# Adding the feed-forward's last bias: four GpSimd additions per group, or one accumulating DMA

## The chip, the core and the metric

The kernel runs on one core of a Trainium2 chip. The core has five engines that run their own instruction streams and wait for each other through semaphores: PE (TensorE, matmuls; its weight loads are listed apart as PEld), DVE (VectorE), ACT (ScalarE), POOL (GpSimd) and SP (SyncE, which here only issues DMAs). Sixteen DMA engines move data between HBM and SBUF. A DMA is issued either by SP, on a queue that the hardware serves, or by POOL, on a queue whose descriptors GpSimd's own software writes. The metric is the device time of one execution in microseconds (us), the median of several runs.

## What is computed

Two layers, each a graph convolution and a feed-forward, over 32 graphs of 512 nodes with 256 features, in float32. The change is in the first layer's feed-forward. Cut to what matters, with `xx` a token's normalized features:

```python
t = max over d of (xx[d] + Wt[f, d]) + bt[f]          # "tropical" product, f = 0..1023
trop = s * max_k(t * sl_cvx + of_cvx) + (1 - s) * min_k(t * sl_ccv + of_ccv)
classical = gelu(xx @ Wc + bc)
g = sigmoid(xx @ Wg + bg)
fused = g * trop + (1 - g) * classical
x = x + (fused @ Wd + bd)
```

The last bias `bd` has 256 numbers. In these inputs they are all zero, and both kernels add them all the same.

## The kernel before

The first layer (`layer0_sorted`) works in four segments of eight graphs, 4096 tokens or 32 tiles of 128 tokens each. Its idea: the maximum over `d` is mostly decided by a token's few largest features. So for each token the graph convolution writes one row to HBM (`rows_of`, 275 numbers: the 256 features, the norm's shift and scale, a count, and the eight largest features with their places). Tokens are then sorted by how many candidates they need. The feed-forward takes the tokens in that order, in groups of four tiles, eight groups per segment, 32 groups in all. Tile number n of a segment looks at `CAPS[n]` candidates: 24, 9, 7, 6, 5, 5, 5, then 4, 3, 2 and 1. Group g takes the tiles g, g+8, g+16 and g+24.

Each group goes through three functions:

- `sums` (from L546) gathers the four tiles' rows into the SBUF tile `xs` (variable `xg`, shape 128 x 4 x 275, three buffers; L553), normalizes the features into `xn` on ACT (L574), turns them on PE for the matmuls, and gathers for each candidate one 4 KB row of the table per token (`best` at L564 for the first candidate, `rows` at L595 for the others). DVE folds each into the running maximum (L598). At its end it compares the counts (`over`, L606) and adds the bias `bd` to the features in `xs`, in four additions on GpSimd, one per tile (L609 and L610). `bd` is a constant in SBUF, the bias repeated in all 128 partitions, loaded once at the start.
- `mixed` does the two matmuls into `cls` and `gate` (L623), their activations (L625) and the mixing of both with the tropical part, on PE, ACT and DVE (L630 to L641).
- `down` multiplies with `Wd` (L652), adds the product on DVE to what stands in `xs` (L654), and stores the features to HBM from SP (`x2s`, L655).

`sums` of a group is woven with `mixed` of the group before, and `down` of that group comes after the first step of the next `mixed`. Beside both runs the graph convolution of the later segments, and in the last segment the start of the second layer. Its work stands on the same engines: on POOL it issues the loads of the adjacency matrix (`adj`, L392) and does small operations for the norms (L30, L31) and copies into the row (L453, L454, L465, L466).

The order of instructions on each engine is not the program's order: the framework simulates the program and puts each engine's instructions in the order in which it expects them to become ready. In the profile the four additions of one group are therefore not next to each other on POOL; gathers and small operations stand between them. A buffer's reuse and every read after a write are guarded by semaphores that the framework places.

The lines that matter: `bd` at L141, `sums` with L553, L564, L574, L595, L598, L606, L609 and L610, and `down` with L654 and L655. The constants are all issued by one helper at L135, so the profile shows that line for them.

Of the kernel before, what the change touches and what calls it, by code (L numbers as in the profile page):

```python
# [8 lines left out]
F32 = mybir.dt.float32  # L9
# [5 lines left out]
ALU = mybir.AluOpType  # L15
# [4 lines left out]
P = 128  # L20
N = 512
D = 256
NT = N // P
# [74 lines left out]
def layer0_sorted(tc, ident, eps, x, adj, w, x2s, ranks, over, following):  # L98
# [6 lines left out]
    nc = tc.nc  # L105
# [22 lines left out]
    with ExitStack() as ctx:  # L128
        cst = ctx.enter_context(tc.tile_pool(name="c0", bufs=1))
        dr = ctx.enter_context(tc.tile_pool(name="d0", bufs=2, space=DRAM))  # L130
        ps = ctx.enter_context(tc.tile_pool(name="p0", bufs=2, space=PSUM))

        def const(name, shape, src):
            t = cst.tile(shape, F32, tag=name, name=name)
            nc.sync.dma_start(t, src)  # L135
            return t
# [1 line left out]
        w_msg = const("w_msg", [P, DC, D], w["W_msg"].rearrange("(c p) u -> p c u", p=P))  # L138
        w_upd = const("w_upd", [P, DC, D], w["W_upd"].rearrange("(c p) u -> p c u", p=P))
        bias = const("bias", [P, D], w["bias"].partition_broadcast(P))  # L140
        bd = const("bd", [P, D], w["bd"].partition_broadcast(P))  # L141
        wc = cst.tile([P, DC, FFN], F32, tag="wc", name="wc")
        wg = cst.tile([P, DC, FFN], F32, tag="wg", name="wg")
        wd = cst.tile([P, FC, D], F32, tag="wd", name="wd")
# [29 lines left out]
        for c in range(CT // P):  # L174
            nc.gpsimd.affine_select(below[:, c, :], below[:, c, :], pattern=[[1, CT]], compare_op=ALU.is_gt,
                                    fill=0.0, base=-c * P, channel_multiplier=-1)

        table = dr.tile([D, FFN], F32, tag="table", name="table", bufs=1)
        least = dr.tile([2, D], F32, tag="least", name="least", bufs=1)
        rows_of = [dr.tile([ST * P, RW], F32, tag=f"rows_of{i}", name=f"rows_of{i}", bufs=1) for i in range(len(x2s))]  # L180
# [362 lines left out]
        def feed_forwards():  # L543


            def sums(s, g):  # L546

                tiles = range(g, ST, NG)
                while s not in placed_segs:
                    next(ahead)  # L550
                xg = sb.tile([P, NT, RW], F32, tag="xs", name=f"xs{s}_{g}", bufs=3)
                for t, tile_no in enumerate(tiles):
                    nc.gpsimd.indirect_dma_start(  # L553
                        out=xg[:, t, :], out_offset=None, in_=rows_of[s],
                        in_offset=bass.IndirectOffsetOnAxis(
                            ap=order[:, s * ST + tile_no : s * ST + tile_no + 1].bitcast(U32), axis=0))
                xnT = sb.tile([P, DC, N], F32, tag="xnT", name=f"xnT{s}_{g}")
                pt = [ps.tile([P, NT, P], F32, tag="tp", name=f"xsp{s}_{g}_{c}") for c in range(DC)]
                best = []

                def ask(t):

                    best.append(sb.tile([P, FFN], F32, tag="best", name=f"best{s}_{g}_{t}", bufs=2 * NT - 1))
                    nc.gpsimd.indirect_dma_start(  # L564
                        out=best[t], out_offset=None, in_=table,
                        in_offset=bass.IndirectOffsetOnAxis(ap=xg[:, t, IDX : IDX + 1].bitcast(U32), axis=0))

                ask(0)
                for t, tile_no in enumerate(tiles):
                    if t + 1 < NT - 1:  # L570
                        ask(t + 1)
                    r, cap = xg[:, t, :], CAPS[tile_no]
                    xn = sb.tile([P, D], F32, tag="xn", name=f"xn{s}_{g}_{t}", bufs=2)
                    nc.scalar.activation(xn, r[:, :D], AF.Identity, bias=r[:, MEAN : MEAN + 1],  # L574
                                         scale=r[:, MEAN + 1 : MEAN + 2])
                    for c in range(DC):
                        nc.tensor.transpose(pt[c][:, t, :], xn[:, c * P : (c + 1) * P], ident)
                    vals, idxs = r[:, VAL : VAL + 8], r[:, IDX : IDX + 8]
                    if cap > 8:
                        rounds = -(-cap // 8)  # L580
                        tops = sb.tile([P, 2, 8 * rounds], F32, tag=f"tops{rounds}", name=f"tops{s}_{g}_{t}", bufs=1)
                        vals, idxs = tops[:, 0, :], tops[:, 1, :]
                        for i in range(rounds):
                            eight = slice(8 * i, 8 * i + 8)
                            nc.vector.max(vals[:, eight], xn)
                            nc.vector.max_index(idxs[:, eight].bitcast(U32), vals[:, eight], xn)
                            if i + 1 < rounds:
                                less = sb.tile([P, D], F32, tag="xn", name=f"less{s}_{g}_{t}_{i}", bufs=2)
                                nc.vector.match_replace(less, vals[:, eight], xn, -3e38)
                                xn = less  # L590
                    m = best[t]
                    nc.scalar.activation(m, m, AF.Identity, bias=vals[:, 0:1])  # L592
                    for k in range(1, cap):
                        row = sb.tile([P, FFN], F32, tag="rows", name=f"rows{s}_{g}_{t}_{k}", bufs=4)
                        nc.gpsimd.indirect_dma_start(  # L595
                            out=row, out_offset=None, in_=table,
                            in_offset=bass.IndirectOffsetOnAxis(ap=idxs[:, k : k + 1].bitcast(U32), axis=0))
                        nc.vector.scalar_tensor_tensor(m, row, vals[:, k : k + 1], m, ALU.add, ALU.max)  # L598
                        if k % 4 == 3:
                            yield  # L600
                    if t == NT - 2:
                        ask(NT - 1)
                    yield
                for c in range(DC):
                    nc.scalar.copy(xnT[:, c, :], pt[c].rearrange("p t n -> p (t n)"))
                nc.vector.tensor_tensor(over[:, s * ST : (s + 1) * ST].rearrange("p (t g) -> p g t", g=NG)[:, g, :],  # L606
                                        xg[:, :, COUNT], limits.rearrange("p (t g) -> p g t", g=NG)[:, g, :],
                                        ALU.is_gt)
                for t in range(NT):  # L609
                    nc.gpsimd.tensor_add(xg[:, t, :D], xg[:, t, :D], bd)  # L610
                got[s, g] = xg, xnT, best

            def mixed(s, g):
# [45 lines left out]
            groups = [(0, NG - 1)]  # L659
            groups += [(s, g) for s in range(len(x2s)) for g in range(NG) if (s, g) != groups[0]]  # L660
            yield from sums(*groups[0])
            for i, now in enumerate(groups):
                steps_ = mixed(*now)
                next(steps_)
                if i:
                    down(*groups[i - 1])
                yield
                more = sums(*groups[i + 1]) if i + 1 < len(groups) else iter(())
                steps = sum(1 + CAPS[n] // 4 for n in range(groups[(i + 1) % len(groups)][1], ST, NG))
                yield from woven(steps_, 9, more, steps)  # L670
# [1487 lines left out]
def tile_kernel(ctx, tc, ins, out):  # L2158
# [21 lines left out]
    with tc.tile_pool(name="few", bufs=1) as few:  # L2180
        over = few.tile([P, n0 + n1], F32, tag="over", name="over")
        NSEG = 4
        x2s = [dram.tile([len(x2) // NSEG * N, D], F32, tag=f"x2s_{i}", name=f"x2s_{i}") for i in range(NSEG)]
        ranks = few.tile([P, len(x2) * NT], I32, tag="ranks", name="ranks")
        rest = []

        def following(ps):
            rest.append(layer1_plain(tc, ident, eps2, x2s, ranks, ins["adj"], w1, out, over[:, n0:], ps))
            return iter(lambda: next(rest[0]), True)

        layer0_sorted(tc, ident, eps2, ins["x"], ins["adj"], w0, x2s, ranks, over[:, :n0], following)
        for _ in rest[0]:
            pass


        ones = few.tile([P, 1], F32, tag="ones", name="ones")
        nc.gpsimd.memset(ones, 1.0)
        worst = few.tile([P, 1], F32, tag="worst", name="worst")
        nc.vector.tensor_reduce(worst, over, AX.X, ALU.add)
        with tc.tile_pool(name="pf", bufs=1, space=PSUM) as ps:  # L2200
            pf = ps.tile([P, N], F32, tag="flag", name="flag")
            nc.tensor.matmul(pf[:1, :1], worst, ones, start=True, stop=True)
            nc.vector.tensor_copy(again, pf[:1, :1])
# [36 lines left out]
```

## Time and profile before

| what | us |
|---|---|
| median of 3 runs | 4451.68 (4451.4 to 4455.35) |
| the profiled execution, its time | 4459.08 |
| the profiled execution, its span (first to last instruction) | 4456.4 |
| first and last start of the additions at L610 | 300.9 and 2300.9 |
| the additions, 128 of 128 x 256 elements: sum | 109.6 |
| mean of one (shortest, median, longest) | 0.861 (0.622, 0.730, 1.777) |
| POOL busy in the whole span | 1718.8 |
| mean granted TensorE clock | 0.948 |

The gathers of the feed-forward, all issued by POOL: `xs` 128 times, `best` 128 times, `rows` 336 times (212 that take their places from `xs`, 124 that take them from `tops`). Their issue takes POOL 1.17 to 1.22 us in the mean; the transfer comes after that.

How to read the profile's lines: a group of instructions is given as line, engine, operation, output<-inputs, shape and count, then busy time in us and the mean of one in ns, then the idle time of the engine just before them and what ended most of it. In the chain of waits each row is a start, a length and an instruction; the chain is followed back from the last instruction to what released it. "issue" is time in which the engine waited for nothing that the profile shows. A DMA is on POOL only while its descriptors are written; its landing is a separate event.

### The profile page before, as it was taken

What the parts mean: (1) busy time and instruction counts of PE and PEld (TensorE: products, weight loads), DVE (VectorE), ACT (ScalarE), POOL (GpSimd) and SP (SyncE); (2) the same over time, 40 slices, a digit from 0 to 9 for tenths busy, and PEclk for the clock granted to TensorE, in tenths of its full rate; (3) what the DMA queues carried; (4) which work ended last, traced back from release to release, by engine and by line L of the source; (5) the groups of instructions that cost most, each with busy time, mean ns of one, the idle gap of its engine ahead of it and who ended that gap; (6) DMA issues with size and microseconds to landing.
All of it is one profiled execution on the core that took longest, in us unless ns stands there. A gap on an engine that the chain in (4) does not pass through costs nothing.

```text
span 4456.4 us, 57911 instructions
## 1 busy us (share of the span) xinstructions
PE 3922.0 (88%) x20311; PEld 2470.6 (55%) x20311; DVE 3347.2 (75%) x7008; ACT 2291.6 (51%) x4756; POOL 1718.8 (39%) x2036
## 2 busy tenths in 40 slices
PE   5568898899988999888997899999999999999987
PEld 4454565566656656545554455555555555555555
DVE  6668887897788987877766777767677877778763
ACT  3345565566564665556654544544545444454433
POOL 2357644664446644454314232332222232332220
PEclk8679999999999999989998999999999999999998
DMA  5546543664436543564422111111111111111100
GB/s 133 160 144 223 190 130 122 210 200 139 156 117 213 187 147 129 162 201 167 138 81 67 36 53 57 56 48 58 51 43 42 53 55 55 58 48 58 41 15 16
DMA packets 235107, 474.21 MB, mean 106 GB/s; under 512 B 38299, under 2 KB 114075, under 8 KB 234804
## 3 DMA queue, kind: packets, MB, share of 16 engines
q0 software_dynamic: 98688, 315.94, 22.2%
q1 hardware_dynamic: 136116, 154.46, 11.0%
q8 instruction: 162, 2.65, 0.2%
q14 instruction: 141, 1.16, 0.1%
HBM read 413.16 MB, written 57.16 MB: 106 GB/s over the span
## 4 chain that ended last, share of the span: by engine, by line
DVE 34%; PE 32%; DMA 11%; issue 9%; POOL 9%; ACT 5%; SPq 0%; POOLq 0%; DVEq 0%; ACTq 0%
DVE att L1213 5%; DVE acc L637 4%; PE clsp L623 3%; PE avp L1249 3%; PE po L652 3%; PE gatep L623 3%; DMA rows<-table,xs 2%; PE yTp L1347 2%; DVE sw L1337 2%; DVE sw L1342 2%; DVE best L598 2%; DMA rows<-table,tops 2%; DVE sst L1340 2%; DMA best<-table,xs 2%; PE xp L1400 1%
## 5 line engine op out<-in xcount | busy, mean ns | idle before, releaser
L623 PE MATMUL clsp<-xnT,wc 128*128 128x512 f32 x1024 | 520.8, 627 | 49.7 <-ACT cls L625 37.6
L623 PE MATMUL gatep<-xnT,wg 128*128 128x512 f32 x1024 | 499.8, 607 | 10.5 <-ACT gate L625 7.7
L652 PE MATMUL po<-wd,acc 128*128 128x256 f32 x2048 | 455.4, 381 | 6.1 <-DVE acc L641 3.8
L1213 DVE SCALAR_TENSOR_TENSOR att<-own,other,mask 128x512 f32<-128x512 f32 x512 | 392.9, 796 | 79.0 <-DMA own<-ownd 79.0
L652 PEld LDWEIGHTS po<-wd,acc 128*128 128x128 f32 x2048 | 388.3, 191 | 72.1 <-issue 9.2
L598 DVE SCALAR_TENSOR_TENSOR best<-rows,xs,best 128x1024 f32<-128x1024 f32 x212 | 274.4, 1295 | 121.9 <-ACT best L592 76.4
L637 DVE SCALAR_TENSOR_TENSOR acc<-past,fld,acc 128x512 f32<-128x512 f32 x448 | 345.7, 775 | 24.9 <-ACT past L636 16.9
L632 ACT ACTIVATE acc<-tz,fld 128x512 f32<-128x512 f32 x256 | 198.8, 777 | 269.3 <-PE tz L630 240.1
L623 PEld LDWEIGHTS gatep<-xnT,wg 128*128 128x128 f32 x1024 | 196.0, 196 | 252.3 <-issue 197.9
L636 ACT ACTIVATE past<-tz,fld 128x512 f32<-128x512 f32 x448 | 291.4, 693 | 68.1 <-DVE acc L637 66.6
L1347 PE MATMUL yTp<-sw,x 128*128 128x512 f32 x512 | 264.6, 655 | 64.3 <-DVE sw L1342 59.6
L595 POOL DMA_INDIRECT rows<-table,xs x212 | 249.5, 1177 | 171.6 <-DVE best L598 119.0
L1249 PE MATMUL avp<-att,hv 128*32 128x512 f32 x2048 | 298.9, 607 | 5.6 <-DVE att L1213 5.6
L623 PEld LDWEIGHTS clsp<-xnT,wc 128*128 128x128 f32 x1024 | 181.5, 198 | 188.1 <-issue 111.8
L434 PE MATMUL pm<-h,adj 128*128 128x258 f32 (+1 forms) x1024 | 181.2, 324 | 99.9 <-DVE keep L427 33.7
L1300 POOL TENSOR_TENSOR mu<-mu,eps 128x16 f32<-128x16 f32 x32 | 111.6, 3487 | 391.1 <-DVE mu L1299 391.0
L1335 PE MATMUL lgp<-wsl,x4T 128*128 128x512 f32 x512 | 242.8, 613 | 15.7 <-ACT sw L1336 6.8
L1154 POOL DMA_INDIRECT x<-x2s,ranks x128 | 135.9, 1062 | 298.1 <-DVE att L1213 148.1
L625 ACT ACTIVATE gate<-gatep,fld 128x512 f32<-128x512 f32 x256 | 175.5, 685 | 142.6 <-PE gatep L623 123.8
L553 POOL DMA_INDIRECT xs<-rows_of,order x128 | 156.1, 1219 | 221.5 <-DVE acc L637 100.8
L1567 PE MATMUL outp<-v,swT 128*128 128x256 f32 x1024 | 227.6, 381 | 0.0
L625 ACT ACTIVATE cls<-clsp,fld 128x512 f32<-128x512 f32 x256 | 176.1, 688 | 93.9 <-PE clsp L623 55.6
(599 smaller groups left out, 8978.1 us busy)
## 6 DMA issues: line engine op xcount, KB each, us to landing
adj<-in_adj POOLq DMA_DIRECT2D x128, 256.0 KB
ai<-in_adj SPq DMA_DIRECT2D x128, 256.0 KB
own<-ownd SPq DMA_DIRECT2D x128, 256.0 KB
rows_of<-keep SPq DMA_DIRECT2D x32, 550.0 KB
x<-in_x SPq DMA_DIRECT2D x32, 512.0 KB
x2s<-xs SPq DMA_DIRECT2D x32, 512.0 KB
out<-x SPq DMA_DIRECT2D x32, 512.0 KB
rows<-table,xs POOLq DMA_INDIRECT x212
```

Source lines behind the costliest of these rows:

```text
L595: nc.gpsimd.indirect_dma_start(out=row, out_offset=None, in_=table, in_offset=bass.IndirectOffsetOnAxis(ap=idxs[:, k : k + 1].bitcast(U32) ...
L598: nc.vector.scalar_tensor_tensor(m, row, vals[:, k : k + 1], m, ALU.add, ALU.max)
L623: nc.tensor.matmul(pf, wf[:, c, f * P : (f + 1) * P], xnT[:, c, :], start=c == 0, stop=c == DC - 1)
L625: nc.scalar.activation(o, pf, fn, bias=fld[:, f, bf : bf + 1], scale=1.0 if fn == AF.Gelu else 0.5)
L636: nc.scalar.activation(r, z, AF.Relu, bias=fld[:, f, AT + b : AT + b + 1])
L637: nc.vector.scalar_tensor_tensor(y, r, fld[:, f, CH + b : CH + b + 1], y, ALU.mult, ALU.add)
L652: nc.tensor.matmul(po[:, i, :], acc[f][:, t * P : (t + 1) * P], wd[:, f, :], start=f == 0, stop=f == FC - 1)
L1213: nc.vector.scalar_tensor_tensor(e, own[h], other[:, j, h : h + 1], mask[:, j, :], ALU.max, ALU.mult)
L1249: nc.tensor.matmul(pv[p][k * HW : (k + 1) * HW, :], hv[:, j, h, e : e + HW], weighed[b, h, j], **ends)
L1335: nc.tensor.matmul(pf, xnT[:, c, t * P : (t + 1) * P], wsl[:, c, :], start=c == 0, stop=c == DC - 1)
L1347: nc.tensor.matmul(py, xn[:, t, c * P : (c + 1) * P], sw[:, t, :], start=t == 0, stop=t == NT - 1)
L1567: nc.tensor.matmul(po[:, :D], swT[:, k, t * P : (t + 1) * P], v[:, k, :], start=k == 0, stop=k == KC - 1)
```

## The change

The bias no longer lies in SBUF. At the start it is copied four times, one below the other, into a small array in HBM (`bd`, 4 x 256, 4 KB). At the end of `sums`, instead of four additions on GpSimd, one DMA is issued on POOL's queue for the whole group. It reads the 4 KB of `bd` once for each of the 128 partitions and adds them, in the DMA engines, to the features of the four tiles in `xs`. The destination is 4 pieces of 256 numbers (1 KB) in each partition, 512 KB in all. The bias is still added in float32 before `down` adds the product.

```diff
         bias = const("bias", [P, D], w["bias"].partition_broadcast(P))
-        bd = const("bd", [P, D], w["bd"].partition_broadcast(P))
...
+        bd = dr.tile([NT, D], F32, tag="bd", name="bd", bufs=1)
+        nc.sync.dma_start(bd, w["bd"].partition_broadcast(NT))
         table = dr.tile([D, FFN], F32, tag="table", name="table", bufs=1)
...
                                         ALU.is_gt)
-                for t in range(NT):
-                    nc.gpsimd.tensor_add(xg[:, t, :D], xg[:, t, :D], bd)
+                nc.gpsimd.dma_start(xg[:, :, :D], bd.partition_broadcast(P), accum_op=ALU.add)
                 got[s, g] = xg, xnT, best
```

## The prediction

> **What bounds the kernel now.** I read the page first: its summary, the slices, the chain.
>
> ```profile
> span 4456.4 us, 57911 instructions
> ...
> PE 3922.0 (88%) x20311; PEld 2470.6 (55%) x20311; DVE 3347.2 (75%) x7008; ACT 2291.6 (51%) x4756; POOL 1718.8 (39%) x2036
> ...
> DMA  5546543664436543564422111111111111111100
> ...
> DVE 34%; PE 32%; DMA 11%; issue 9%; POOL 9%; ACT 5%; SPq 0%; POOLq 0%; DVEq 0%; ACTq 0%
> ```
>
> No engine bounds the whole. The chain of waits goes back and forth between DVE and PE, with 11% in transfers and 9% on POOL. The additions run only in the gathered feed-forward, from 300.9 to 2300.9 us, and there the DMA engines are about half busy. Next, the groups of instructions on POOL:
>
> ```profile
> L610 POOL TENSOR_TENSOR xs<-xs,bd 128x256 f32<-128x256 f32 x128 | 109.6, 861 | 169.9 <-ACT xn L574 168.9
> L392 POOL DMA_DIRECT2D adj<-in_adj x128 | 71.6, 575 | 16.1 <-DVE own_part L169 9.7 <-issue 5.1
> ```
>
> The 128 additions (32 groups of four) cost POOL 109.6 us, and POOL stands 168.9 us in front of them for `xn`. POOL is busy 42 to 59% of this stretch, by its parts (253 of 600 us at the end, 253 of 430 at the start), so that is time on an engine with slack. What an addition is worth is read from the chain, here in one late group:
>
> ```profile
> 2220.20 0.94 POOL best L564
> 2221.15 0.66 POOL xs L610
> 2221.81 3.62 issue
> ...
> 2225.66 1.11 POOL rows L595
> ...
> 2229.14 5.45 DMA rows<-table,xs
> ```
>
> The fourth addition stands between the last `best` gather and the `rows` gathers, but 3.62 us of waiting follow it (POOL's timeline says: for DVE's `best`, L598), so even here its 0.66 us isn't missed. The landing of the last `rows` gather, 5.45 us, does set the pace. Busy time by stretch shows how full the DMA engines are around that place:
>
> ```profile
> 2216.00:2225.00 9.00, 8.97 (x35) 6.09 (x34) 2.98 (x4) 5.92 (x10) 4.88 (x5) 1.00 0.72 225
> 2225.00:2228.00 3.00, 3.00 (x16) 2.64 (x15) 2.93 (x3) 2.19 (x2) 2.04 (x2) 1.00 0.08 29
> 2228.00:2235.00 7.00, 7.00 (x35) 5.82 (x34) 4.79 (x6) 0.87 (x2) 1.85 (x2) 1.00 0.68 225
> 860.00:885.00 25.00, 21.17 (x82) 13.05 (x82) 21.39 (x40) 12.34 (x20) 18.24 (x19) 0.93 0.84 273
> ```
>
> Columns: length, busy time of PE, PEld, DVE, ACT, POOL, clock, DMA share, GB/s. Between the burst of four `best` gathers and that of the `rows` gathers lies a hole of 3 us with the DMA engines at 0.08. In a group with many gathers (860 to 885 us, tiles with caps up to 24) there is no hole: 0.84 for 25 us. Last, the timeline of DVE beside an addition:
>
> ```profile
> 2209.50 0.75 DVE L637 SCALAR_TENSOR_TENSOR acc<-past,fld,acc 128x512 f32<-128x512 f32 x1 [0.75 <-ACT past L636]
> 2210.03 0.80 POOL L610 TENSOR_TENSOR xs<-xs,bd 128x256 f32<-128x256 f32 x1 [9.93 <-ACT xn L574]
> 2210.28 1.10 DVE L639 TENSOR_TENSOR acc<-acc,cls 128x512 f32<-128x512 f32 x1
> ```
>
> L639 takes 1.10 us beside the addition and 0.69 elsewhere. I took every DVE instruction that overlaps an addition (230) and summed what each took beyond the median of its kind while POOL was idle: 45.7 us. The same sum is 23.1 us for the 728 indirect DMA issues in this stretch and 2.3 us for the 128 plain ones.
>
> **What the Trainium skill says.** SBUF — State Buffer, Who interferes with whom: a DVE instruction with two SBUF inputs contends with a GpSimd instruction that reads SBUF, not with one that only writes. The trace agrees: 45.7 us of lengthened DVE work by 128 additions, 2.3 us by 128 plain issues. DMA: Bandwidth & Descriptors, SWDGE vs HWDGE vs iDMA: accumulating is possible only in DMAs issued by GpSimd. So the new DMA joins the queue that carries all gathers, behind those issued before it and ahead of those after; q0 is that queue in the page, 315.94 MB of 474.21. Collectives: The Full Stack, The bandwidth ceiling: an add in the DMA engines isn't slow by its arithmetic, but by two source reads for each chunk, measured at 62.28 against 32.35 GB/s, a factor of 1.93. No transfer here accumulates, so the trace can neither confirm nor deny it. Perfetto Trace Analysis, Per-instruction lifecycle: the end of a GpSimd DMA in the profile is the end of descriptor writing, not of the movement; so the 575 ns of L392 are a price for POOL alone.
>
> **The change part by part.** The sums are made against the profiled execution: span 4456.4 us, time 4459.08. That is 7.4 us above the median of the runs, 4451.68; I add the difference to the median.
>
> *Additions removed.* Of the 128, pieces of 25 stand on the chain between 270 and 2310 us, 13.1 us together: −13.1.
>
> *Issues added.* 32 accumulating issues on POOL, each 4 x 256 elements in 128 partitions, so 512 pieces of 1 KB. Lower bound: L392's 0.575 us, with 128 pieces. Upper bound: four times that, 2.3 us, if the cost goes by pieces. I take 1.2 us, since the issue has a fixed part that the trace doesn't separate. About 8 of the 25 pieces on the chain are a group's last addition, where the issue will stand: 8 x 1.2 = +9.6 (bounds 4.6 and 18.4).
>
> *DVE freed.* 45.7 us, weighed with DVE's share of the chain's pieces between 270 and 2310 us, 31.2%: −14.3. Bounds: 0, if another wait is just as late, and −45.7, if DVE paces everything.
>
> *The transfer.* A 1,024-byte packet on the hardware queue takes 46 ns at the median (58,880 of them). Each of 16 engines gets 512/16 = 32 packets: 1.47 us as a plain copy, 32 x 46 x 1.93 = 2.84 us with the second read (an estimate from the packets and Collectives). The lower bound is 1.47. The upper bound is 6.4 us: 32 packets at the 200 ns that a 4,096-byte packet of the gathers takes on average. I take 2.84. Eight groups, the first two of each of four segments (caps 24 and 9), have no hole, so each pays in full: +22.7. In the other 24 the hole of about 3 us takes it where the order is as above; where hole and transfer don't meet, the gather behind it lands later. Software-queue share in these stretches is about 0.4, and half of such a delay is covered: 24 x 0.4 x 2.84 x 0.5 = +13.6.
>
> *Waits.* One DMA waits for all four `xn` (L574), where each addition waited for its own. Queued behind it on POOL are this group's `rows` gathers, the next group's `xs`, the `adj` loads and the small norm operations (L30, L31); DVE waits for the norms and ACT for the gathers. The fourth addition already stood there, and of the 168.9 us only 38.3 were followed by an operation that then started at once (within 0.32 us), so I cost this at 0. The bounds: 38.3 us weighed with the share of DVE and POOL in the chain's pieces, 39.6%, makes −15 and +15. The reader of the sum is DVE's L654, a group (some 50 us) later: landing is hidden there. The bias's copy into DRAM is one 4 KB transfer on SP beside the first loads, and the load of 128 KB into SBUF that it replaces took SP 0.43 us: 0, hidden behind 270 us of other work.
>
> *Order.* The additions of one group aren't contiguous on POOL: other operations stand between them, so the order is planned from expected readiness, and it will shift on all engines. I see no sign in it. No row prices it; as what moves is what stands around these additions, I give it the bounds of the waits, ±15.
>
> Sum: −13.1 + 9.6 − 14.3 + 22.7 + 13.6 = +18.5. 4451.7 + 18.5 = 4470.2 us.
>
> **The rivals.** *Faster: the holes swallow the transfer.* If the engines take at most the hole, 3 us, and it begins in it, light groups pay nothing, and heavy ones half because ACT and DVE still work on earlier rows: +11. With a cheap issue (+4.6) and DVE's relief at half its 45.7 (−23): 11 + 4.6 − 13.1 − 23 = −20.5, 4431 us. For it: DVE leads the chain, and the hole is measured. Against it: 25 us without a hole in the heavy groups.
>
> *No change.* Only the heavy groups pay: 18.5 − 13.6 = +4.9, 4457 us. For it: every term is small against the ±15 of the order.
>
> *Much slower: the accumulating packets are slow.* At 200 ns a transfer lasts 6.4 us, more than twice the hole. Heavy groups: 8 x 6.4 = 51; light ones: 24 x (6.4 − 3) x 0.6 = 49; less the relief of 17.8 (13.1 + 14.3 − 9.6): +82, 4534 us. For it: each packet must fetch its old values before it can write, and nothing in this trace does that. Against it: the factor of 1.93. It decides from the point where a transfer outlasts the hole of 3 us.
>
> *It does not unload GpSimd.* At 2.3 us or more an issue, POOL wins 109.6 − 73.6 = 36 us at most, against 91 us at 0.575; this moves the sum by 9 us and changes no sign.
>
> **How the numbers follow.** What can be told from no change is about 0.2%, 8.9 us. Forecast (slower by 9 to 45 us): 0.38, own range 4461 to 4497. Much slower: 0.12. No change: 0.20. Faster: 0.30. So slower 0.50, same 0.20, faster 0.30. The range leaves a tenth on each side: down to 4425, past the faster case by part of the order's ±15, and up to 4535, the slow packets' case.
>
> **What would show it.** Right: 32 issues on L610's place at 0.6 to 2.3 us; L637, L639, L640 and L641 at a mean some 20 to 30 ns shorter; the chain with fewer pieces of DVE and more of `rows` and `best` landings; a longer stretch in the heavy groups. Packets of the new DMA at 85 to 95 ns each confirm the factor; 46 or 200 decide for a rival. Wrong: DVE's instructions as long as before, or the gathers after an accumulating DMA landing in the same 5.45 us, or POOL waiting in front of the new DMA for something other than `xn`.

## The result, and the profile after

The changed kernel takes 4436.4 us (median of 6 runs, 4426.63 to 4439.12) where the kernel before takes 4455.17 us on the same chip: a ratio of 0.9948, with a 95% interval of 0.9937 to 0.996. By the ratio it is 23 us faster; the two medians lie 18.8 us apart. 4470 us had been forecast, 18.5 us slower. The profiled execution of the changed kernel has a time of 4439.12 us, a span of 4437.4 us and a mean granted clock of 0.949 (0.948 before).

The page of the changed kernel, the same rows as shown of before (span; busy time of each engine; busy tenths of the DMA engines in 40 slices; the chain's shares by engine):

```profile
span 4437.4 us, 57823 instructions
...
PE 3911.4 (88%) x20311; PEld 2467.2 (56%) x20311; DVE 3302.7 (74%) x7008; ACT 2290.5 (52%) x4756; POOL 1646.4 (37%) x1940
...
DMA  4547644675446644565522111111111111111100
...
PE 34%; DVE 28%; DMA 10%; issue 8%; POOL 7%; ACT 5%; SPq 0%; POOLq 0%; DVEq 0%; ACTq 0%
```

POOL is 72.4 us less busy, which says little about the time, since POOL had slack. DVE is 44.5 us less busy with the same 7008 instructions, and its share of the chain fell from 34% to 28%. The share of transfers did not rise: 10%, after 11%.

The groups of instructions of the changed kernel: the new DMA, and two of DVE's groups (busy time and mean in ns, then the idle time before them).

```profile
L610 POOL DMA_DIRECT2D xs<-bd x32 | 44.9, 1402 | 79.0 <-ACT xn L575 55.9 <-issue 13.2 <-ACT cls L625 9.4
...
L637 DVE SCALAR_TENSOR_TENSOR acc<-past,fld,acc 128x512 f32<-128x512 f32 x448 | 332.4, 744 | 29.9 <-ACT past L636 21.7 <-DVE deg L439 0.4
L639 DVE TENSOR_TENSOR acc<-acc,cls 128x512 f32<-128x512 f32 x256 | 174.9, 684 | 22.1 <-ACT acc L632 19.0 <-ACT gate L625 1.4 <-issue 0.5
```

L637 had a mean of 775 ns before, L639 one of 705. DVE's timeline beside one of the new DMAs, which is on POOL from 2186.64 to 2188.08 us, shows the same in single instructions:

```profile
2186.35 0.74 DVE L637 SCALAR_TENSOR_TENSOR acc<-past,fld,acc 128x512 f32<-128x512 f32 x1
...
2187.61 0.68 DVE L639 TENSOR_TENSOR acc<-acc,cls 128x512 f32<-128x512 f32 x1
```

Before, an L639 beside an addition took 1.10 us. Summed as in the prediction, against the median of each kind while POOL is idle, the DVE instructions beside the additions were 45.7 us too long; those beside the new DMAs are 0.5 us too short, which is nothing. So DVE gained what the prediction had counted as the most that it could gain. The 23.1 us that the prediction summed beside the indirect issues came from instructions that overlapped an addition as well: before the change, the 1145 DVE instructions that overlap an indirect issue and nothing else on POOL are 1.3 us too short in sum.

Now where the DMA stands. POOL's timeline in a late part of the feed-forward, before and after:

```profile
2197.72 1.04 POOL L595 DMA_INDIRECT rows<-table,xs  x1 [0.31 <-issue]
2198.78 1.31 POOL L610 TENSOR_TENSOR xs<-xs,bd 128x256 f32<-128x256 f32 x2
2210.03 0.80 POOL L610 TENSOR_TENSOR xs<-xs,bd 128x256 f32<-128x256 f32 x1 [9.93 <-ACT xn L574]
...
2220.20 0.94 POOL L564 DMA_INDIRECT best<-table,xs  x1 [0.30 <-issue]
2221.15 0.66 POOL L610 TENSOR_TENSOR xs<-xs,bd 128x256 f32<-128x256 f32 x1
```

```profile
2185.68 0.95 POOL L596 DMA_INDIRECT rows<-table,xs  x1 [0.30 <-issue]
2186.64 1.44 POOL L610 DMA_DIRECT2D xs<-bd  x1
2200.57 1.04 POOL L565 DMA_INDIRECT best<-table,xs  x1 [12.49 <-PE tz L630]
```

The addition at 2221.15 us is the second of its group, not the fourth: counted in fours, the 128 additions put the pair at 2198.78 us at the end of group 30 and those at 2210.03 and 2221.15 us at the beginning of group 31, whose last two follow at 2250.80 us, behind later row gathers. So the DMA, which needs all four `xn`, came to stand behind the last row gather, and POOL issues nothing for 12.49 us after it. In that stretch the DMA engines are not idle, but PE and DVE are nearly full (columns: length, busy PE, PEld, DVE, ACT, POOL, clock, DMA share, GB/s):

```profile
2188.00:2200.50 12.50, 11.97 (x39) 6.09 (x40) 11.70 (x18) 8.30 (x14) 0.08 (x1) 1.00 0.47 111
```

The chain of the changed kernel, in the late group that follows, still has the same landing in it:

```profile
2204.94 0.94 POOL best L565
2205.88 4.41 issue
...
2210.51 1.11 POOL rows L596
...
2212.68 5.12 DMA rows<-table,xs
```

5.12 us, where 5.45 were shown before. It is not longer. That row gather is issued 22 us after the DMA, whose packets are over by then. Counted over all groups, the packets of the DMA are over before POOL issues its next gather in 21 of 32. The other 11 include seven of the eight heavy groups; there the next gather is issued 0.3 to 0.4 us behind the DMA.

What the transfers did to the gathers as a whole is read from the idle time in front of the instructions that consume them: DVE's folding of rows, and ACT's first touch of `best`. Before:

```profile
L598 DVE SCALAR_TENSOR_TENSOR best<-rows,xs,best 128x1024 f32<-128x1024 f32 x212 | 274.4, 1295 | 121.9 <-ACT best L592 76.4 <-DMA rows<-table,xs 43.3
L598 DVE SCALAR_TENSOR_TENSOR best<-rows,tops,best 128x1024 f32<-128x1024 f32 x124 | 164.0, 1322 | 38.2 <-DMA rows<-table,tops 31.4 <-ACT best L592 6.3
L592 ACT ACTIVATE best<-best,xs 128x1024 f32<-128x1024 f32 x120 | 136.6, 1146 | 125.2 <-DMA best<-table,xs 124.4
```

After:

```profile
L599 DVE SCALAR_TENSOR_TENSOR best<-rows,xs,best 128x1024 f32<-128x1024 f32 x212 | 271.0, 1280 | 126.3 <-ACT best L593 77.9 <-DMA rows<-table,xs 46.4
L599 DVE SCALAR_TENSOR_TENSOR best<-rows,tops,best 128x1024 f32<-128x1024 f32 x124 | 158.5, 1279 | 39.6 <-DMA rows<-table,tops 35.3 <-ACT best L593 3.6
L593 ACT ACTIVATE best<-best,xs 128x1024 f32<-128x1024 f32 x120 | 136.2, 1145 | 108.1 <-DMA best<-table,xs 106.0 <-DMA adj<-in_adj 0.7
```

DVE waits 7.0 us more for landing rows (46.4 + 35.3 against 43.3 + 31.4), ACT 18.4 us less for landing `best`. The cleaner comparison is a kernel with neither additions nor DMA (run no_bias, below):

```profile
L597 DVE SCALAR_TENSOR_TENSOR best<-rows,xs,best 128x1024 f32<-128x1024 f32 x212 | 271.1, 1280 | 124.8 <-ACT best L591 76.0 <-DMA rows<-table,xs 46.7
L597 DVE SCALAR_TENSOR_TENSOR best<-rows,tops,best 128x1024 f32<-128x1024 f32 x124 | 158.7, 1280 | 39.5 <-DMA rows<-table,tops 34.2 <-ACT best L591 5.0
L591 ACT ACTIVATE best<-best,xs 128x1024 f32<-128x1024 f32 x120 | 136.2, 1146 | 115.5 <-DMA best<-table,xs 114.3
```

The three waits make 195.2 us here and 197.3 in a second profile of it; in two profiles of the changed kernel they make 187.7 and 197.1. The 36.3 us of later landings that the prediction had charged are not there.

### The profile page after: what moved, and what is told of

It is laid out like the page before. It is cut to its first block, busy times and chain, and to the rows that moved or that the text cites. A ratio compares the mean times of both kernels' runs of the same rounds, so it can differ in the third digit from the quotient of the medians.

```text
span 4437.4 us, 57823 instructions
## 1 busy us (share of the span) xinstructions
PE 3911.4 (88%) x20311; PEld 2467.2 (56%) x20311; DVE 3302.7 (74%) x7008; ACT 2290.5 (52%) x4756; POOL 1646.4 (37%) x1940
## 4 chain that ended last, share of the span: by engine, by line
PE 34%; DVE 28%; DMA 10%; issue 8%; POOL 7%; ACT 5%; SPq 0%; POOLq 0%; DVEq 0%; ACTq 0%
DVE att L1213 5%; PE clsp L623 4%; PE gatep L623 4%; PE po L652 4%; PE avp L1249 3%; DVE acc L637 3%; PE yTp L1347 2%; DVE sw L1337 2%; DMA rows<-table,xs 2%; DVE best L599 2%; DVE sw L1342 2%; DMA rows<-table,tops 2%; DVE sst L1340 2%; DMA best<-table,xs 2%; PE oTp L1535 1%
## 5 line engine op out<-in xcount | busy, mean ns | idle before, releaser
L599 DVE SCALAR_TENSOR_TENSOR best<-rows,xs,best 128x1024 f32<-128x1024 f32 x212 | 271.0, 1280 | 126.3 <-ACT best L593 77.9
L637 DVE SCALAR_TENSOR_TENSOR acc<-past,fld,acc 128x512 f32<-128x512 f32 x448 | 332.4, 744 | 29.9 <-ACT past L636 21.7
L636 ACT ACTIVATE past<-tz,fld 128x512 f32<-128x512 f32 x448 | 290.7, 694 | 65.6 <-DVE acc L637 65.2
L435 PEld LDWEIGHTS pm<-h,adj 128*128 128x128 f32 x1024 | 151.8, 214 | 129.1 <-issue 68.2
```

Source lines behind the costliest of these rows:

```text
L435: nc.tensor.matmul(pm[:, : c1 - c0], a[:, i, t * P : (t + 1) * P], h[:, i, c0:c1], start=i + c0 == 0, stop=i + 1 == NT and c0 > 0)
L636: nc.scalar.activation(r, z, AF.Relu, bias=fld[:, f, AT + b : AT + b + 1])
L637: nc.vector.scalar_tensor_tensor(y, r, fld[:, f, CH + b : CH + b + 1], y, ALU.mult, ALU.add)
```

## The experiments

The theories: R, that the gain comes from GpSimd no longer reading SBUF beside DVE; P, that it comes from POOL having less to do; O, that it comes from the one wait and the order of instructions that comes with it. Then, since the added DMA cost much less than forecast: H, that the transfers are cheap because of their place; C, that they are cheap wherever they stand; T, that what they do cost lies in the transfer; W, that it lies in one more instruction and wait on POOL's queue. Each run is compared with the kernel before on the same chip; diffs are against the kernel that is named.

### One addition for each group (against the kernel before)

```diff
-                for t in range(NT):
-                    nc.gpsimd.tensor_add(xg[:, t, :D], xg[:, t, :D], bd)
+                nc.gpsimd.tensor_add(xg[:, :, :D], xg[:, :, :D], bd.unsqueeze(1).to_broadcast([P, NT, D]))
```

> The kernel before with one GpSimd addition of 128 x 4 x 256 per group in place of four. POOL's order becomes that of the changed kernel, with the addition where the DMA stands. Theory R (the gain is DVE freed[...]): the reads are still there, so DVE's lengthening stays at 30 to 45 us and the time at 4447 to 4458 us, close to before. Theory O (the gain is one instruction with one wait in a later place, and the order that follows): 4430 to 4441 us, as with the DMA. Theory P (the gain is POOL's time): about 30 of the 65 us that POOL won, so 4444 to 4450 us, with no lengthening of DVE needed.

Measured: 4475.71 us, ratio 1.0043 (1.0028 to 1.0057): 19 us slower than before. The groups of this run:

```profile
L609 POOL TENSOR_TENSOR xs<-xs,bd 128x1024 f32<-128x1024 f32 x32 | 73.7, 2304 | 78.8 <-ACT xn L574 78.3
L636 DVE SCALAR_TENSOR_TENSOR acc<-past,fld,acc 128x512 f32<-128x512 f32 x448 | 354.0, 793 | 31.5 <-ACT past L635 23.4 <-ACT acc L631 0.4
```

It has the changed kernel's single wait for four `xn`, its addition has the same neighbours on POOL as the DMA in 30 of 32 groups, and it has 35.9 us less of additions (73.7 against 109.6); yet it loses. O falls, and P as the main cause. R had not expected so much either (4447 to 4458 us). DVE's L636 is longer than before the change (793 against 775 ns), and the sum over all DVE instructions beside an addition is 56.1 us, of which 39.0 us lie on the chain, against 45.7 and 22.7 us before. The time follows DVE: the 16.3 us more on the chain are most of the 19.

### Reads put back behind the DMA (against the changed kernel)

```diff
+        spare = cst.tile([P, D], F32, tag="spare", name="spare")
...
-                nc.gpsimd.dma_start(xg[:, :, :D], bd.partition_broadcast(P), accum_op=ALU.add)
+                added = nc.gpsimd.dma_start(xg[:, :, :D], bd.partition_broadcast(P), accum_op=ALU.add)
+                with tc.issue_after(added.ins):
+                    for t in range(NT):
+                        nc.gpsimd.tensor_add(spare, bias, bias)
```

> The changed kernel with four GpSimd additions more per group, placed on POOL behind the accumulating DMA, that read and write only spare data (128 x 256, the size of the old additions); no one waits for them. R: DVE's lengthening comes back, 30 to 45 us, and the time with it: 4446 to 4462 us. P: the same time, but DVE's instructions keep their length. O: 4433 to 4441 us, as the additions stand in no wait of the feed-forward.

Measured: 4470.11 us, ratio 1.0035 (1.0021 to 1.0048), some 39 us more than the changed kernel's ratio gives, and above the range that R had given.

```profile
L614 POOL TENSOR_TENSOR spare<-bias 128x256 f32<-128x256 f32 x128 | 126.3, 987 | 4.7
...
L641 DVE SCALAR_TENSOR_TENSOR acc<-past,fld,acc 128x512 f32<-128x512 f32 x448 | 341.0, 763 | 30.2 <-ACT past L640 22.2 <-DVE deg L440 0.4
```

### Writes instead of reads (against the changed kernel)

The run above with `spare` and the loop's body replaced (the diff is against that run):

```diff
-        spare = cst.tile([P, D], F32, tag="spare", name="spare")
+        spare = cst.tile([P, 3 * D], BF16, tag="spare", name="spare")
...
-                        nc.gpsimd.tensor_add(spare, bias, bias)
+                        nc.gpsimd.memset(spare, 0.0)
```

> The changed kernel with four GpSimd memsets more per group (128 x 768 in bf16, each about as long as an addition), placed as in the kernel with the spare additions: POOL has the same work, but reads nothing. R: DVE keeps its length and the time stays at 4430 to 4442 us. P: 4446 to 4462 us, as with the spare additions. O: 4433 to 4441 us.

Measured: 4439.52 us, ratio 0.9967 (0.9955 to 0.9979).

```profile
L614 POOL MEMSET spare<- 128x768 bf16 x128 | 117.5, 918 | 2.5
...
L641 DVE SCALAR_TENSOR_TENSOR acc<-past,fld,acc 128x512 f32<-128x512 f32 x448 | 332.5, 745 | 30.1 <-ACT past L640 22.5
```

The two runs occupy POOL about equally long in the same place (126.3 and 117.5 us). The reads lengthen DVE's work by 39.2 us and take back more than the gain; the writes lengthen it by nothing (−0.7 us), and most of the gain stays, with POOL busier than before the change (1731.2 against 1718.8 us). The reads alone are thus worth 30 us (1.0035 less 0.9967). R holds as the main cause. POOL's time may not be free: the memsets stand some 10 us above the changed kernel (0.9967 against 0.9945, the mean of its two measurements, with intervals that overlap), so P may keep a part of about that size.

### Without any bias (against the kernel before), twice

The last bias is left out: neither additions nor the DMA, nor the load of `bd`.

```diff
-        bd = const("bd", [P, D], w["bd"].partition_broadcast(P))
...
-                for t in range(NT):
-                    nc.gpsimd.tensor_add(xg[:, t, :D], xg[:, t, :D], bd)
```

> The kernel before without the bias: neither additions nor DMA nor its load; the last bias is left out of the computation. It prices the accumulating DMA, by the difference to the changed kernel. Theory H (the transfers fall into holes of the DMA engines): 4429 to 4439 us, as the changed kernel. The prediction's price (22.7 and 13.6 us for transfers, 9.6 for issues): 4388 to 4402 us.

> The kernel without additions, DMA and bias (the last bias is left out) once more, for a tighter price of the changed kernel's DMA. Theory C (the transfers cost next to nothing): ratio to the kernel before 0.992 to 0.994, that is 3 to 10 us under the changed kernel. Theory T (the transfers and issues cost the 46 us that the prediction gave them, and the relief of DVE is as much larger): 0.984 to 0.986.

Measured: 4423.46 us, ratio 0.993 (0.9908 to 0.9951), and 4419.94 us, ratio 0.9917 (0.9899 to 0.9935). The first lies between H's range and that of the prediction's price, the second just under C's and far from T's. Taking the additions away is thus worth 31 to 37 us, and what the changed kernel pays back for its DMA is the rest: 23 us were gained at the first measurement, 26 us at the next one (below), so the price is about 10 us (34 less 24.5). The intervals leave several us on either side. The prediction had 45.9 us: with the gain of 23 us that would have needed a ratio of 0.985 here, and the second of these runs has 0.9899 as its lower end.

### The changed kernel again, and the DMA put where the prediction had it

The first is the changed kernel as it is, as a measure. In the second, a group's DMA is kept back and issued right behind the third `best` gather of the next group, ahead of that group's row gathers:

```diff
+        unbiased = []
+
+        def add_bias():
+            done = unbiased.pop()
+            nc.gpsimd.dma_start(done[:, :, :D], bd.partition_broadcast(P), accum_op=ALU.add)
...
+                    if t == NT - 2 and unbiased:
+                        with tc.issue_after(asked.ins):
+                            add_bias()
...
-                nc.gpsimd.dma_start(xg[:, :, :D], bd.partition_broadcast(P), accum_op=ALU.add)
+                unbiased.append(xg)
```

> The changed kernel itself, once more, as the measure for the three that run beside it. Every theory expects what it gave the first time, a ratio of 0.9948 (about 4433 us where the kernel before has 4456).

> The changed kernel with each group's accumulating DMA issued one group later in its place among the gathers: right behind the third best gather of the next group and so ahead of that group's row gathers, where the prediction had put it. Theory H (the transfers are cheap because they fall in a hole of some 12 us that the prediction read as 3 us): put ahead of the row gathers they push these back by a transfer of 3.3 us or so in each of 32 groups, part of it hidden: 15 to 35 us slower than the changed kernel, ratio to the kernel before 0.998 to 1.003. Theory C (a transfer of this size costs next to nothing wherever it stands, since row gathers are asked for early enough): as the changed kernel within 5 us, ratio 0.994 to 0.996.

Measured: 4427.83 us, ratio 0.9942 (0.9923 to 0.996), and 4422.8 us, ratio 0.9942 (0.992 to 0.9965). H, which expected 15 to 35 us more, falls: the place makes no difference that can be measured, with intervals of some 9 us to either side. POOL's timeline of the second in a late group shows how even this place can be harmless:

```profile
2194.86 0.94 POOL L571 DMA_INDIRECT best<-table,xs  x1 [0.30 <-issue]
2195.81 1.44 POOL L548 DMA_DIRECT2D xs<-bd  x1
2200.52 1.98 POOL L605 DMA_INDIRECT rows<-table,xs  x1 [3.28 <-DVE best L608]
2202.80 0.98 POOL L605 DMA_INDIRECT rows<-table,xs  x1 [0.30 <-issue]
```

The row gather behind the DMA waits 3.28 us for DVE (`best`, L608) anyhow, so the DMA's issue and the first part of its transfer run in a wait that exists without it. The packets of this DMA run from 1.5 to 6.5 us after its issue ends; the row gather is issued 3.3 us after it. Over all groups, the packets are over before the next gather's issue in only 10 of 32 here, where the changed kernel had 21.

### A quarter of the transfer (against the changed kernel)

The bias is added to a group's last tile only, that of the other three is left out.

```diff
-                nc.gpsimd.dma_start(xg[:, :, :D], bd.partition_broadcast(P), accum_op=ALU.add)
+                nc.gpsimd.dma_start(xg[:, NT - 1 :, :D], bd[:1].partition_broadcast(P), accum_op=ALU.add)
```

> The changed kernel with the bias added to the last of a group's four tiles only: 128 KB in 128 pieces instead of 512 KB in 512; the bias of the other three tiles is left out. Theory T (what the changed kernel loses against one without the bias is the transfer and the longer issue): three quarters of it goes, 4425 to 4429 us where the kernel before has 4456, ratio 0.993 to 0.994. Theory W (what it loses is the fixed part: one more instruction and one more wait on GpSimd's queue in each group): as the changed kernel, 4433 to 4438 us. Should the changed kernel be within 5 us of the one without the bias, the two can't be told apart here. Mean issue expected: 0.6 us, as a gather of 128 pieces has it, against 1.40 us for 512.

Measured: 4427.69 us, ratio 0.993 (0.9906 to 0.9955). That is where T expected it, but the interval takes in the changed kernel's 0.9942 too. With so little to divide, the run does not settle between T and W. It does give a price of the issue, 0.96 us, where 0.6 had been expected:

```profile
L610 POOL DMA_DIRECT2D xs<-bd x32 | 30.8, 964 | 78.0 <-ACT xn L575 77.6
```

### Four DMAs of a tile each (against the changed kernel)

```diff
-                nc.gpsimd.dma_start(xg[:, :, :D], bd.partition_broadcast(P), accum_op=ALU.add)
+                for t in range(NT):
+                    nc.gpsimd.dma_start(xg[:, t, :D], bd[0].partition_broadcast(P), accum_op=ALU.add)
```

> The changed kernel with one accumulating DMA for each tile (128 KB in 128 pieces) instead of one for the group: the same packets, four issues of 0.96 us (the mean that the run on one tile showed) instead of one of 1.40 us: 78 us more of GpSimd's time over 32 groups. If GpSimd's own time in this place counts (8 of 32 on the chain, as the prediction took): 20 us more than the changed kernel, ratio 0.998 to 1.000. If it is free, as the run with memsets behind the DMA suggests: 0.994 to 0.996.

Measured: 4437.23 us, ratio 0.9955 (0.9939 to 0.997).

```profile
L611 POOL DMA_DIRECT2D xs<-bd x128 | 124.3, 1012 | 161.0 <-ACT xn L575 159.5 <-issue 0.7
```

POOL spends 79.4 us more on issues than in the changed kernel (124.3 against 44.9), and the time moves by about a thousandth, within the intervals. The prediction's rate, a quarter of the issues on the chain, would have made 20 us of it. Little of POOL's own time reaches the total here.

### Three times the transfer (against the changed kernel)

Two more accumulating DMAs behind each group's own, into tensors in DRAM that nobody reads.

```diff
+        spare = [dr.tile([P, NT, D], F32, tag=f"spare{i}", name=f"spare{i}", bufs=1) for i in range(2)]
...
-                nc.gpsimd.dma_start(xg[:, :, :D], bd.partition_broadcast(P), accum_op=ALU.add)
+                added = nc.gpsimd.dma_start(xg[:, :, :D], bd.partition_broadcast(P), accum_op=ALU.add)
+                with tc.issue_after(added.ins):
+                    for i in range(2):
+                        nc.gpsimd.dma_start(spare[i], bd.partition_broadcast(P), accum_op=ALU.add)
```

> The changed kernel with two more accumulating DMAs of 512 KB behind the group's own, into tensors in DRAM that nobody reads: three times the packets and issues on the queue of the gathers, nothing more on DVE or in SBUF. If each transfer and issue costs what the prediction took (45.9 us for 32 of them), 92 us more than the changed kernel, ratio near 1.015. If they are covered by the distance to the next gathers and by the work of the group before (theory C), two of them still reach past the cover in part, since three lie 10 to 15 us one after another where the next best gathers are 12 us off: 10 to 40 us more, ratio 0.996 to 1.003. If the cover holds even so: 0.994 to 0.996.

Measured: 4472.45 us, ratio 1.0028 (1.0014 to 1.0042): some 37 us more than the changed kernel (0.0083 of 4460), or 0.58 us for each of the 64 added DMAs. The prediction's price was 45.9 / 32 = 1.43 us for one. The packets differ (128 of 4 KB for each DMA, 328 ns at the median, 8 x 328 ns = 2.6 us for each engine, against 32 x 102 ns = 3.3 us for the bias), so the comparison is of like size, not exact. The first DMA of a group costs 10 / 32 = 0.3 us by the times, but 0.56 us by the stores (below), so it isn't settled whether it is cheaper than the next two.

```profile
L614 POOL DMA_DIRECT2D spare<-bd x64 | 75.1, 1413 | 0.0
```

These issues occupy POOL for about as long as those that the run with four DMAs added (75.1 and 79.4 us), and that run, on the same chip, has a ratio of 0.9955. By this comparison some 33 of the 37 us (1.0028 less 0.9955) come with the transfers, not with POOL's time. They don't show as later landings of `best`: ACT waits 126.8 us for them here and 106.0 in the changed kernel, but 126.1 with the DMA moved, 125.3 with a quarter of it and 130.1 with four DMAs, and none of these is slower by more than its interval. What grows here are the waits for `x`, the rows that the graph convolution loads through SP's queue: 63.9 us, against 47.7 and 48.2 in the changed kernel and 38.5 and 41.5 without any bias. That points to followers that the prediction didn't list; the run with the DMA moved, with 34.0 us at the changed kernel's ratio, speaks against it as the whole answer, and no run isolates it.

### The bias in TensorE's accumulation (against the kernel before)

A version meant to beat both: the bias as the first term of the down product, a row of ones times the bias row.

```diff
-        bd = const("bd", [P, D], w["bd"].partition_broadcast(P))
+        bd = cst.tile([1, D], F32, tag="bd", name="bd")
+        nc.sync.dma_start(bd, w["bd"].rearrange("(o n) -> o n", o=1))
...
+        oner = cst.tile([1, P], F32, tag="oner", name="oner")
+        nc.gpsimd.memset(oner, 1.0)
...
-                for t in range(NT):
-                    nc.gpsimd.tensor_add(xg[:, t, :D], xg[:, t, :D], bd)
...
+                        nc.tensor.matmul(po[:, i, :], oner, bd, start=True, stop=False)
                         for f in range(FC):
                             nc.tensor.matmul(po[:, i, :], acc[f][:, t * P : (t + 1) * P], wd[:, f, :],
-                                             start=f == 0, stop=f == FC - 1)
+                                             start=False, stop=f == FC - 1)
```

> Neither additions nor a DMA: the bias goes in as the first term of the down product's accumulation, one matmul of one row of ones by the bias row for each tile, 128 matmuls of 256 columns. If TensorE's added time stands on the chain in full, with some 0.23 us each (the mean that the down product's matmuls of 256 columns have), it is 29 us above the kernel without a bias, near 4453 us, and no better than the changed kernel; if a third of it does, as TensorE's share of the chain has it, near 4433 us, a tie with the changed kernel; if it fills waits, near 4424 us and ahead of it. Expected: 4433 us, ratio 0.995. DVE busy as in the changed kernel, 3300 us.

Measured: 4467.27 us, ratio 1.0029 (1.0017 to 1.0042), slower than both.

```profile
PE 3978.2 (89%) x20567; PEld 2475.5 (55%) x20567; DVE 3310.3 (74%) x7008; ACT 2286.1 (51%) x4756; POOL 1606.9 (36%) x1909
...
L652 PE MATMUL po<-bd,oner 1*128 1x256 f32 x256 | 89.6, 429 | 2.8 <-DVE h L411 2.7
```

The expectation's price was wrong by a factor of three. Each of these matmuls leaves two records, so 128 of them are 256 records and 89.6 us, not 29. Here a product over one row took as long as one over 128: the 256 records have a mean of 429 ns, those of the down product itself 392. PE is 78 us busier than without a bias (3978.2 against 3900.2), and the time about 47 us longer (1.0029 against 0.9924, the mean of the two runs), although the granted clock of its profiled execution was higher (0.961 against 0.954 and 0.953).

### How the difference builds up

The times at which each group's features are stored (`x2s`, L655) in the profiled executions: before in us, the others as the difference from it. Two values are two profiles of the same kernel.

| store of group | before | changed | without bias | three DMAs |
|---|---|---|---|---|
| 1 | 424.6 | +1.1, +8.7 | −0.4, +5.7 | +2.6 |
| 8 | 907.6 | −8.0, −1.4 | −15.3, −7.3 | +2.7 |
| 16 | 1439.7 | −9.2, −5.3 | −25.1, −16.9 | +11.1 |
| 24 | 1957.5 | −8.9, −4.2 | −37.2, −23.7 | +29.1 |
| 32 | 2376.1 | −19.1, −21.3 | −44.6, −36.1 | +17.9 |

From the first store to the last, the changed kernel gains 20 and 30 us, the one without a bias 44 and 42. By this measure the DMA costs 18 us (43 less 25) and not 10, with single profiles behind it; both figures are far below 45.9. The distance between the changed kernel and the one without a bias grows over the groups up to the 24th and is no single event.

## Why the prediction was wrong, point by point

**What failed: the step called the transfer, +22.7 and +13.6.** It priced each accumulating DMA as if the next gather were waiting behind it and as if that gather's landing then set the pace: in full in eight groups, and at two fifths and one half in the other 24. The measured price of all 32 DMAs, issues included, is 10 us by the times and 18 us by the stores, against 45.9 us in the sum. Two readings led there. The place was taken from a chain that doesn't tell the four additions of a group apart: the one at 2221.15 us was called the group's fourth and is its second. And a high share of busy DMA engines in the heavy groups (0.84) was read as no room at all. The DMA put back into the predicted place shows that the first error by itself cost nothing that can be measured (0.9942 in both places). What failed is the second half of the step, that a gather behind the DMA lands later and that this is paid in time. The sign that the prediction had named for being wrong is what came: the same landing, 5.12 us for 5.45, and waits for `rows` and `best` no longer than without any DMA (187.7 and 197.1 against 195.2 and 197.3 us).

In most groups the trace shows the reason: a `rows` gather follows a wait for DVE, a `best` gather one for PE (`tz`, 12.49 us), and the transfer runs during these waits. The prediction named such a wait, 3.62 us for L598, used it to call the addition free, and did not apply it to the transfer. In seven of the eight heavy groups there is no such wait; the next gather does follow at once, as the prediction supposed, and what takes up the transfer there no run isolates.

**DVE freed, −14.3; additions removed, −13.1.** The mechanism was right; together they were put at 27.4 us and measured 31 to 37 us by the runs without a bias. What was too small is the weight. The 45.7 us were multiplied by DVE's mean share of the chain, 31.2%. Of the lengthened instructions themselves, 116 of the 230 stood on the chain, with 22.7 of the 45.7 us: half (21 to 28 us, depending on how one counts an instruction that the chain covers in part). With that, 13.1 + 22.7 = 35.8 us, within what was measured. The same sum, POOL's own pieces on the chain and the lengthened work of DVE there, was formed afterwards for three runs. One addition for each group: 10.2 + 39.0 = 49 us, where the run is 53 us above those without a bias. Spare additions: 19.3 + 20.6 = 40 us, where it is 40 above the changed kernel. Memsets: 7.6 − 0.4 = 7 us, where it is 10. The measured figures have some 7 us to either side, so this supports the weighing and doesn't prove it. Here the mean share of an engine undersold the relief.

**Issues, +9.6.** One issue takes 1.402 us, where 1.2 was taken between bounds of 0.575 and 2.3. But the weight was too high: not 8 but 3 of the 32 issues stand on the changed kernel's chain, with 3.3 us, and 79 us more of them in the run with four DMAs moved the time by no more than its interval.

**The packets.** 1,024-byte packets of the new DMA take 102 ns at the median, against 46 ns for plain ones on the hardware queue: a factor of 2.2. The factor of 1.93 from the Trainium skill's page Collectives: The Full Stack, The bandwidth ceiling, had given 89 ns. The measured factor is the larger one; a part of it may be the queue's, since plain packets of 2 KB take 99 ns on the software queue and 84 on the hardware queue. So the transfer was priced a little too low by itself, 2.84 for 3.3 us on each engine, and the error in the total has the other sign. The rival of slow packets at 200 ns is out.

**Waits and order, 0 each.** POOL waits 55.9 of 79.0 us in front of the DMA for `xn`, the rest for an issue and for `cls`. The run with one addition had the same wait and nearly the same order without the DMA, and most of its loss is accounted for by DVE. No sign of either was found, and within about 10 us none could be excluded.

**The rivals.** The faster one was right in its sign and near in its number, 4431 us, in part by luck: its reason, the hole of 3 us, was not the one, and its charge of 11 us for the heavy groups has no run behind it. Its half of DVE's relief, 23 us, is what the chain shows. No change, 4457 us, is out by the interval of the ratio. "It does not unload GpSimd": it does, by 72.4 us, and this is not where the time comes from.

**Reads and writes.** SBUF — State Buffer, Who interferes with whom, a page of the Trainium skill, held in the strict form that it states: reads by GpSimd lengthen DVE's work on two SBUF inputs (39.2 us for 128 additions on unrelated data), writes by it do not (−0.7 us for 128 memsets). Before the change, the 25 statistics of one input (L40, L445) that overlap an addition are 0.03 us too long in sum.

**Left open.** What takes up the transfer in the heavy groups. What the remaining 10 to 18 us of the DMA consist of, transfer or one more instruction and wait in POOL's queue: the quarter and the four DMAs differ from the changed kernel by less than their intervals. The changed kernel's waits for `x`, some 8 us longer than without a bias, are a hint and no more. And why the last eight groups gain another 7 to 17 us against the kernel before, in the changed kernel and in those without a bias and with three DMAs alike: no run isolates it.

## What to carry to other kernels

GpSimd work that reads SBUF beside DVE cost this kernel more by what it did to DVE than by GpSimd's own time. To price such work, sum the lengthened DVE instructions and count those that stand on the chain, instead of weighing them with DVE's mean share. Before charging an added transfer with late landings, look up for each follower what it already waits for and how long, loads on other queues included. A high share of busy DMA engines did not mean that an added transfer was paid for in full. And tell the copies of an instruction apart by counting them, since in a planned order neighbours in time may belong to different groups.

## What the runs showed of the hardware

- In these runs 32 GpSimd additions of 1024 elements per partition disturbed DVE more than 128 of 256: 56.1 us of lengthened DVE work against 45.7, although GpSimd itself was faster (73.7 against 109.6 us).
- Issuing DMAs on GpSimd did not lengthen DVE's work: −1.3 us for the 1145 instructions beside indirect issues alone, −0.5 us for those beside the new DMAs.
- The issue of an accumulating DMA from GpSimd takes 0.96 to 1.01 us for 128 pieces of 1 KB and 1.40 us for 512, so, as an estimate, (1.402 − 0.964) / 3 = 0.15 us for each 128 pieces above a fixed part of about 0.8 us. The plain loads of `adj` with 128 pieces took 0.58 to 0.70 us in these runs.
- Accumulating packets of 1 KB into SBUF took 102 ns at the median, those of 4 KB into DRAM 328 ns; the plain 4 KB packets of the gathers, on the same queue, 159 ns.
- A float32 matmul over one row of 256 columns took as long as one over 128 rows (two records with a mean of 429 ns, against 392).
